# Two-layer graph attention: layer 1's exponentials made in layer 0 and read back from DRAM, and list work reordered

## The chip, the cores and the metric

The kernel runs on one core of a Trainium2 chip. The metric is the device time of one launch in microseconds; before the change the median of 3 runs is 1829.27 us (1828.33 to 1834.35). The engines are named as in the profile: PE (TensorE, matrix products; PEld its weight loads), DVE (VectorE), ACT (ScalarE), POOL (GpSimd) and SP (SyncE, which here only issues DMAs).

## What is computed

The input is a feature matrix `x` of 3327 x 1024 and a sparse symmetric adjacency matrix `adj` of 3327 x 3327 with its diagonal set. Two layers of graph attention follow one another, each with a residual and a layer norm:

```python
# layer 0: 8 heads of 128 columns
h = (x @ W0).reshape(C, 8, 128)
e = alpha_src[:, :, None] + alpha_dst[:, None, :]      # per head, from h . a_src and h . a_dst
e = where(e >= 0, e, 0.2 * e);  e = where(adj == 0, -inf, e)
x = layernorm(x + softmax(e) @ h)
# layer 1: one head of 1024 columns
h = x @ W1;  f1 = h @ a1;  f2 = h @ a2
e = leaky_relu(f1 + f2.T, 0.2);  scores = where(adj > 0, e, -9e15)
x = layernorm(x + relu(softmax(scores, axis=1) @ h))
```

The exponential of a leaky sum is split: up to a factor that cancels in the softmax, the weight of source j for target i is max(r_i * a_j, b_j), with r_i = exp(0.8 s_i), a_j = exp(d_j) and b_j = exp(0.2 d_j). So each layer needs one r for each target (and head), and two numbers for each source.

## The kernel before, in words

The 3327 rows are padded to 26 tiles of 128 (`NT`, `P`). There are three stages.

**Projections and lists** (the first block under `manual_schedule`). For each tile, `flip` transposes x on PE, `project` multiplies it by W0 in three column chunks (`CUTS0`), `keep` evicts the chunks on ACT and stores the tile's rows, with their source factors appended, to `h0_d` in DRAM. Beside it the generator `listing` turns each tile's adjacency rows into lists of neighbours: for each tile 17 columns of 128 source indices and target numbers (`idx`, `tgt`), four blocks of four groups and an end block. One round of `listing` works on several tiles at once: `keys` and `columns` (DVE) for tile t+1, `give`, `take` and `sources` (PE, ACT, DVE) for tile t, `ends` and `ends2` for tile t+3, and `count(t + 4)`, which clears the diagonal of a tile's mask on POOL (L342), sums the mask on ACT (L346), packs it on DVE (L353), and requests a later mask from POOL's queue (L531). `pace`, called after every second step of a projection, advances `listing` by a fixed quota (`slots`), and from tile 13 on also `sums_so_far`, which makes part of layer 0's sums for the first 13 tiles. Since the program is written in a fixed order, every engine takes its instructions in the order in which these generators emit them.

**Layer 0** (`pipeline` with `Layer0` items; tiles 13 to 25 alternate with tiles 0 to 12). A late item has blocks 0 to 4, an early one blocks 2 to 4. For each block POOL issues four indirect DMAs (one for the end block) that gather 128 rows each from `h0_d` into a ring of five buffers; `weights` makes the block's weights on DVE (L1093, L1094, L1098) and a copy on ACT (L1096); `sums` multiplies on PE (L1129; L1118 for the end block). `own` adds the target's own row: an Exp on ACT (L1065), three DVE operations (L1066 to L1068), then eight operations on ACT for late items (L1076) or on DVE for early ones (L1072). `finish` is a generator of five steps: the denominators (DVE L1151, PE L1152), the division and residual (L1155 to L1161), the layer norm (`norm_steps`: bn_stats L217, the square root on ACT L220, L224), and two dot products (L1168) that give layer 1's scores, whose exponentials (ACT L1173, L1174) are appended to the row before it goes to `y_d` in DRAM (SP, L1175).

**Layer 1** (`Target` items, in order of tiles). A block is again four gathers, now from `y_d`, the weights on DVE (L1223, L1224, L1226) and products on PE in three column chunks (L1235). `prepare` is called for the next item in the middle of the current one: it transposes the target scores on PE (L1191), takes their Exp on ACT (L1193), makes the marks on DVE (L1033, L1037) and requests the residual rows (SP, L1198). The transposed scores, their exponentials and the products of DVE all lie in one PSUM tile, `way`. `own` takes a second Exp of the same scores by column (L1204). `close` divides (L1249, L1252); `finish` transposes the result on PE with a copy on ACT (`turned`, L199), multiplies by W1 (L1267) and adds the residual (L1270), and `settle` is the layer norm with the store.

The table `plans` says which unfinished items advance after each block. A pair such as (2, 1) means: one step of the item two back, then one step of the item one back; the entry in front is for the start of an item, before its own work is emitted.

Of the kernel before, what the change touches and what calls it, by code (L numbers as in the profile page):

```python
# [14 lines left out]
OP = mybir.AluOpType  # L15
# [11 lines left out]
def kernel(  # L27
# [97 lines left out]
    idx = const.tile([P, NT, NB], I32, name="idx")  # L125
    tgt = const.tile([P, NT, NB], F32, name="tgt")
    wt1 = const.tile([P, KT, D], F32, name="wt1")
    half_d = [scratch.tile([P, D], F32, name=f"half_d{t}") for t in range(EARLY)]
    dens = const.tile([P, EARLY, H], F32, name="dens")
    io_t = const.tile([P, P], F32, name="io_t")  # L130
# [183 lines left out]
    class Edges:  # L314
# [10 lines left out]
        def factors(self):  # L325
# [6 lines left out]
            nc.gpsimd.tensor_copy(mv[:, 1, :], r[:, 1, :])  # L332
            nc.gpsimd.tensor_tensor(mv[:, 2, :], r[:, 1, :], mv[:, 1, :], OP.subtract)

        def words(self, ad, junk):

            sbuf, ph, t = self.ph.sbuf, self.ph, self.t  # L340
            own = ad[:, t * P : (t + 1) * P].bitcast(mybir.dt.int8)
            nc.gpsimd.affine_select(  # L342
                out=own, in_=own, pattern=[[1, P]], compare_op=OP.not_equal, fill=0.0, base=0, channel_multiplier=-1
            )
            for n in range(2):
                nc.scalar.activation(junk, ad[:, n * THR : (n + 1) * THR], AF.Copy, accum_out=self.d[:, n : n + 1])  # L346
            self.deg_b = sbuf("deg_b", [P, 2], 4, dt=BF16)
            nc.scalar.activation(self.deg_b, self.d, AF.Copy)
            w = ad.bitcast(I32)
            for n in range(3):  # L350
                m = WD >> n
                half = sbuf(f"wd{n}", [P, m], 4 if n == 2 else 1, dt=I32)
                nc.vector.scalar_tensor_tensor(  # L353
                    half, w[:, m:], 1 << n, w[:, :m], op0=OP.logical_shift_left, op1=OP.bitwise_or
                )
                w = half
            self.bytes = w.bitcast(U8)
# [152 lines left out]
    with ExitStack() as own, tc.manual_schedule():  # L510
# [39 lines left out]
        def keep(t, c):  # L550
# [12 lines left out]
            if kept[t] == 3:  # L563
                nc.sync.dma_start(h0_d[t * P : (t + 1) * P, :HW0], hts.pop(t))

        def count(t):
            if t < NT:
                lists[t].words(ads.pop(t), junk)
                if t:
                    load_mask(t + 2)  # L570

        def listing():

            for t in range(-1, NT):
                old, new = lists[t] if t >= 0 else None, lists[t + 1] if t + 1 < NT else None
                for s in range(4):
                    if old and s:
                        old.give(s - 1)
                    if new:
                        (new.keys, new.columns)[s // 2](s % 2)  # L580
                    if s == 1 and 2 < t + 3 < NT:
                        lists[t + 3].ends(tri_b)
                    if s == 3 and 2 < t + 3 < NT:
                        lists[t + 3].ends2(all_b)
                    yield
                if old:
                    old.give(EB - 1)
                    old.give(EB)
                    old.take()
                if new:  # L590
                    new.ways()
                count(t + 4)
                yield
                if old:
                    old.sources()
                    yield
                while new and t + 1 not in scored:
                    yield
                if new:
                    new.places()  # L600
                    yield
                    new.spread()
                    yield

        scored, kept, soon = set(), {}, []
        steps, slots, done = listing(), [0, 0], [0]

        def pace():
# [214 lines left out]
        )  # L823
        all_b = pool.tile([P, P], BF16, bufs=1, name="all_b")
        nc.vector.tensor_copy(all_b, tri)
        count(0)
        for _ in range(2):
            next(steps)
# [8 lines left out]
        project(1, 2, False)  # L837
        keep(1, 2)
        lists[0].ends2(all_b)
        lists[1].ends(tri_b)  # L840
        flip(3, 0)
        load_x(5)
        count(2)

        done[0], slots[:] = 4, [9, (NT - 3) * 12 + 13]
        project(2, 2, True, lambda: flip(3, 1))
        keep(2, 2)
        flip(4, 0)
        lists[1].ends2(all_b)
        lists[2].ends(tri_b)  # L850
        project(3, 2, True, lambda: flip(4, 1))
        keep(3, 2)
        lists[2].ends2(all_b)
        for t in range(3, NT):
            load_x(t + 3)
# [27 lines left out]
                )  # L883
            if t == NTH:
                soon.append(sums_so_far())
            for c in (0, 1):
                project(t, c)
                keep(t, c)
            if t + 2 < NT:
# [65 lines left out]
    def sparse(own):  # L955
# [3 lines left out]
        srcs = near + [pool.tile([P, NG, HG], F32, bufs=1, name=f"src{n}") for n in range(HB, NS)]  # L959
        ends = [pool.tile([P, 1, HG], F32, bufs=1, name=f"end{n}") for n in range(2)]  # L960
        r1 = Rows(pool, 1)

        ys = [pool.tile([P, HW], F32, bufs=1, name=f"y{n}") for n in range(3)]
        for y in ys:
# [75 lines left out]
        class Layer0:  # L1040
# [107 lines left out]
            def finish(self):  # L1148
# [23 lines left out]
                        yield  # L1172
                nc.scalar.activation(row[:, D + 1 : D + 2], r1.d[:, t, :], AF.Exp)  # L1173
                nc.scalar.activation(row[:, D + 2 : D + 3], r1.d[:, t, :], AF.Exp, scale=SLOPE)  # L1174
                nc.sync.dma_start(y_d[t * P : (t + 1) * P, :HW], row)  # L1175
                stored.add(t)

        class Target:

# [7 lines left out]

            def prepare(self):
                t = self.t
                tr = way[:, 3 * P :]  # L1190
                nc.tensor.transpose(tr, r1.s[:, t, :].to_broadcast([P, P]), ident)  # L1191
                self.r = way[:, ((t + 1) % 2) * P : ((t + 1) % 2 + 1) * P].rearrange("p (g t) -> p g t", g=NG)
                nc.scalar.activation(  # L1193
                    self.r.rearrange("p g t -> p (g t)"), tr, AF.Exp, scale=1 - SLOPE
                )
                self.oh, self.oh2 = marks(t)
                self.res = ys[self.n % 3]
                nc.sync.dma_start(self.res, y_d[t * P : (t + 1) * P, :HW])  # L1198

            def own(self):  # L1200

                t, res = self.t, self.res
                es = self.es = sbuf("es1", [P, 2], 2)
                nc.scalar.activation(es[:, 1:], r1.s[:, t, :], AF.Exp, scale=1 - SLOPE)  # L1204
                nc.vector.scalar_tensor_tensor(
                    es[:, 1:], res[:, D + 1 : D + 2], es[:, 1:], res[:, D + 2 : D + 3], op0=OP.mult, op1=OP.max
                )
                nc.vector.tensor_tensor(es[:, :1], es[:, 1:], loop[:, t : t + 1], OP.mult)

# [70 lines left out]
        def pipeline(items, fetches):  # L1280

            left, sums_of, sent = [], set(), [0]
            plans = {
                len(Target.blocks): ((), (1,), (1,), (1,), (1,), (1,)),
                len(Target.blocks) - HB: ((), (1, 1), (1, 1), (1,)),
                Target: ((2,), (2, 1), (2, 1), (1, 1), (1, 1), (1,)),
            }

# [32 lines left out]
            for i, it in enumerate(items):  # L1321
# [4 lines left out]
                for j, b in enumerate(it.blocks):  # L1326
                    if j == 0 and i:
                        items[i - 1].close()
                        if turn:
                            for _ in left[i - 1]:  # L1330
                                pass
                            send()
                            it.weights(b)
                        rest(i, 0)
# [185 lines left out]
```

## Time and profile before

| | us |
|---|---|
| median of 3 runs | 1829.27 |
| profiled execution, its own time | 1945.79 |
| span of its instructions | 1944.1 |
| PE busy | 1633.7 (84% of the span) |
| DVE busy | 1184.5 (61%) |
| POOL busy | 1092.2 (56%) |
| ACT busy | 573.4 (29%) |
| table loads on ACT: L220 / L1173 / L1193 | 50, 26 and 23 of 1.283 each |
| indirect DMAs (POOL) | 884, about 1 each |

The profile is of one execution, which took 1945.79 us, 6% more than the median of the timed runs. Its page gives the span in 40 equal slices (48.6 us each), each digit the busy share of an engine in tenths; `PEclk` is the share of full speed that PE's clock was granted, `DMA` the mean busy share of the core's 16 DMA engines. A row of a group has the line, the engine, the operation and its tiles, the count, busy time and mean duration, then the engine's idle time ahead of it and what ended it. In a timeline a row has its start in us, its duration in us, and in brackets how long the engine had been idle and what released it. Line numbers are those of the kernel before. Idle time of an engine that sets no end costs nothing.

### The profile page before, as it was taken

The page shows a single profiled execution, that of the slowest core. Times are in us where ns is not written, and L with a number is a line of the kernel's source. Part 1 is how long each engine was busy: PE and PEld are TensorE (multiplying, and loading weights), DVE is VectorE, ACT ScalarE, POOL GpSimd, SP SyncE. Part 2 cuts the span into 40 slices and gives each one's busy share as a digit, 9 for nine tenths or more (in the row PEclk, how much of TensorE's full clock was granted, in tenths as well). Part 3 has the DMA queues.
Part 4 walks back from the last instruction along what each step waited for, and adds up shares of the span by engine and source line. Part 5 has one row for each costly group of instructions (what it writes and reads, how often), then busy time and mean ns, then how long its engine had stood idle before and what let it go on. Part 6 is the DMA issues. An engine that isn't in the chain of part 4 may idle for free.

```text
span 1944.1 us, 35431 instructions
## 1 busy us (share of the span) xinstructions
PE 1633.7 (84%) x13168; PEld 919.9 (47%) x13168; DVE 1184.5 (61%) x3261; ACT 573.4 (29%) x1565; POOL 1092.2 (56%) x1580
## 2 busy tenths in 40 slices
PE   8699989989994777777777665798989999899988
PEld 5466556655563554554455442243434434333433
DVE  6699988777765776777777774243444344434342
ACT  5656554444321222222222121022122221222121
POOL 4433346656555666666666555565656666565640
PEclk9899999999996878888878877899999999999999
DMA  6555779887779999999999998899999999899980
GB/s 178 91 130 114 144 152 293 255 249 238 247 271 349 381 391 393 383 393 371 402 386 386 374 313 301 310 374 340 346 350 369 335 394 342 331 362 340 325 302 33
DMA packets 183364, 585.16 MB, mean 301 GB/s; under 512 B 36168, under 2 KB 42824, under 8 KB 183182
## 3 DMA queue, kind: packets, MB, share of 16 engines
q0 software_dynamic: 131056, 457.74, 68.4%
q1 hardware_dynamic: 52126, 125.06, 17.2%
q8 instruction: 107, 1.75, 0.4%
q14 instruction: 75, 0.61, 0.1%
HBM read 586.09 MB, written 51.22 MB: 328 GB/s over the span
## 4 chain that ended last, share of the span: by engine, by line
PE 43%; issue 10%; DVE 6%; ACT 4%; DMA 4%; POOL 1%; another core or an unknown queue 0%; DVEq 0%; ACTq 0%; POOLq 0%
PE mm L1267 17%; PE acc L1235 13%; PE acc L1129 8%; PE acc L1110 2%; DMA src<-h_d,idx 2%; PE tr L196 1%; ACT L1193 1%; PE acc L1118 1%; DVE e L1098 1%; ACT own L1076 1%; DMA near<-h_d,idx 1%; DVE pr L982 1%; DVE st L217 1%; ACT L220 1%; DMA src<-y_d,idx 1%
## 5 line engine op out<-in xcount | busy, mean ns | idle before, releaser
L542 PE MATMUL mm<-wt,xT 128*128 128x347 f32 (+1 forms) x1248 | 416.6, 475 | 6.8 <-ACT ht L561 3.3
L1267 PE MATMUL mm<-wt,xT 128*128 128x512 f32 x832 | 395.5, 613 | 2.6 <-issue 2.3
L1017 POOL DMA_INDIRECT src<-y_d,idx x248 | 249.1, 1005 | 166.8 <-PE acc L1235 71.0
L542 PEld LDWEIGHTS mm<-wt,xT 128*128 128x128 f32 x1248 | 228.5, 195 | 118.3 <-issue 19.7
L1017 POOL DMA_INDIRECT src<-h_d,idx x184 | 196.5, 1068 | 121.3 <-PE acc L1129 35.8
L1267 PEld LDWEIGHTS mm<-wt,xT 128*128 128x128 f32 x832 | 152.3, 193 | 211.5 <-issue 206.7
L1270 DVE SCALAR_TENSOR_TENSOR o<-mm,y 128x512 f32<-128x512 f32 x52 | 36.0, 692 | 322.2 <-PE acc L1235 126.4
L1017 POOL DMA_INDIRECT near<-y_d,idx x168 | 169.5, 1009 | 108.7 <-PE acc L1235 48.3
L1129 PE MATMUL acc<-src,e 128*32 128x128 f32 x2944 | 161.3, 324 | 52.1 <-issue 47.5
L1017 POOL DMA_INDIRECT near<-h_d,idx x120 | 130.6, 1088 | 82.4 <-PE acc L1129 31.0
L1235 PE MATMUL acc<-src,es 128*32 128x341 f32 x1488 | 130.6, 485 | 41.8 <-DVE es L1226 31.8
L1129 PEld LDWEIGHTS acc<-src,e 128*32 128x32 f32 x2944 | 111.5, 130 | 113.4 <-issue 93.8
L1098 DVE TENSOR_TENSOR e<-oh,way 128x1024 f32<-128x1024 f32 x104 | 127.1, 1222 | 59.3 <-ACT w L1096 43.1
L1129 PE MATMUL acc<-near,e 128*32 128x128 f32 x2048 | 116.0, 333 | 48.7 <-issue 34.8
L199 ACT ACTIVATE xT<-tr 128x512 f32<-128x512 f32 x104 | 62.1, 598 | 299.9 <-PE tr L196 151.6
L1129 PEld LDWEIGHTS acc<-near,e 128*32 128x32 f32 x2048 | 79.7, 133 | 93.7 <-issue 84.4
L1096 ACT ACTIVATE w<-way 128x32 f32<-128x32 f32 x104 | 20.3, 195 | 351.4 <-DVE way L1094 186.6
L1249 ACT ACTIVATE z<-y,ri 128x342 f32<-128x342 f32 (+1 forms) x78 | 39.5, 569 | 277.0 <-issue 121.6
L1235 PE MATMUL acc<-near,es 128*32 128x342 f32 (+1 forms) x1008 | 85.8, 469 | 21.3 <-DVE es L1226 14.0
L629 POOL DMA_INDIRECT near<-h_d,idx x76 | 82.1, 1080 | 31.5 <-issue 22.9
L1235 PEld LDWEIGHTS acc<-src,es 128*32 128x32 f32 x1488 | 44.4, 114 | 115.0 <-issue 61.1
L346 ACT ACTIVATE junk<-ad 128x1664 uint8<-128x1664 uint8 x52 | 83.8, 1611 | 16.2 <-POOL ad L342 14.8
(242 smaller groups left out, 2587.8 us busy)
## 6 DMA issues: line engine op xcount, KB each, us to landing
h_d<-ht SPq DMA_DIRECT2D x26, 520.0 KB
own<-h_d SPq DMA_DIRECT2D x26, 520.0 KB
y_d<-y SPq DMA_DIRECT2D x26, 514.0 KB
y<-y_d SPq DMA_DIRECT2D x26, 514.0 KB
x<-in_x_dram SPq DMA_DIRECT2D x25, 512.0 KB
y<-in_x_dram SPq DMA_DIRECT2D x25, 512.0 KB
out_dram<-o SPq DMA_DIRECT2D x25, 512.0 KB
ad<-in_adj_dram POOLq DMA_DIRECT2D x25, 415.9 KB
```

The source lines that it names most:

```text
L199: nc.scalar.activation(part, tr, AF.Copy)
L346: nc.scalar.activation(junk, ad[:, n * THR : (n + 1) * THR], AF.Copy, accum_out=self.d[:, n : n + 1])
L542: nc.tensor.matmul(acc, xT[t][:, k, :], wt[:, k, CUTS0[c] : CUTS0[c + 1]], start=k == 0, stop=k == KT - 1)
L629: nc.gpsimd.indirect_dma_start(out=src[n % 3][:, g, :], out_offset=None, in_=h0_d[:THR, :], in_offset=bass.IndirectOffsetOnAxis(ap=idx[:, ...
L1017: nc.gpsimd.indirect_dma_start(out=s[:, g, :w], out_offset=None, in_=table[:n, :], in_offset=bass.IndirectOffsetOnAxis(ap=idx[:, t, b * NG ...
L1098: nc.vector.tensor_tensor(e, oh.unsqueeze(2).to_broadcast([P, ng, H, wide]), wp.unsqueeze(3).to_broadcast([P, ng, H, wide]), OP.mult,)
L1110: nc.tensor.matmul(self.acc[j - 1].rearrange("p h d -> p (h d)"), ident, self.h[:, (j - 1) * HALF : j * HALF], start=False, stop=False,)
L1129: nc.tensor.matmul(self.acc[h // 4][g * GT : (g + 1) * GT, h % 4, :], e[:, g, h, :], rowsof[:, g, h, :], start=first and h % 4 == 0, stop= ...
L1235: nc.tensor.matmul(self.acc[c][to, :m], es[:, g, :], s[:, g, CUTS[c] : CUTS[c + 1]], start=b == 0, stop=b == EB,)
L1249: nc.scalar.activation(z[:, cut], self.res[:, cut], AF.Copy, scale=ri[:, 1:2])
L1267: nc.tensor.matmul(acc, xT[:, k, :], wt1[:, k, half], start=k == 0, stop=k == KT - 1)
L1270: nc.vector.scalar_tensor_tensor(o[:, half], acc, 0.0, res[:, half], op0=OP.max, op1=OP.add)
```

## The change

It has two halves. First, `r`, the exponential of the target scores of layer 1, is made in layer 0. `finish` of a `Layer0` item takes the Exp by column into a kept tile `grow`, and gains a sixth step: PE transposes that column (broadcast over 128 columns), ACT copies one row of the result to SBUF, and SP stores it as one line of 512 bytes, `row_d[t]`, in DRAM. In layer 1, `prepare` reads that line back into all 128 partitions with one DMA, in place of the transpose L1191 and the Exp L1193, and `own` reads `grow` in place of the Exp L1204. The tile `r` thereby moves from PSUM (`way`) to SBUF (`rr`). The plans call the sixth step at the start of an item, for the item two back.

Second, in the list work, the clearing of a mask's diagonal leaves `words` and becomes `clear`, emitted for tile t+4 with the third of a round's first four steps (and for tiles 0 to 2 at the start); `count(t + 4)` moves from the middle of a round to its end; `places` and `spread` share a step; the first projections of tile 3 and some `ends` are emitted in another order, with the pacing quota set to match.

```diff
--- before.py
+++ after.py
@@ -125,6 +125,7 @@
     idx = const.tile([P, NT, NB], I32, name="idx")
     tgt = const.tile([P, NT, NB], F32, name="tgt")
     wt1 = const.tile([P, KT, D], F32, name="wt1")
+    row_d = [scratch.tile([1, P], F32, name=f"row_d{t}") for t in range(NT)]
     half_d = [scratch.tile([P, D], F32, name=f"half_d{t}") for t in range(EARLY)]
     dens = const.tile([P, EARLY, H], F32, name="dens")
     io_t = const.tile([P, P], F32, name="io_t")
@@ -332,16 +333,19 @@
             nc.gpsimd.tensor_copy(mv[:, 1, :], r[:, 1, :])
             nc.gpsimd.tensor_tensor(mv[:, 2, :], r[:, 1, :], mv[:, 1, :], OP.subtract)
 
-        def words(self, ad, junk):
-
-
-
-
-            sbuf, ph, t = self.ph.sbuf, self.ph, self.t
-            own = ad[:, t * P : (t + 1) * P].bitcast(mybir.dt.int8)
+        def clear(self, ad):
+
+            own = ad[:, self.t * P : (self.t + 1) * P].bitcast(mybir.dt.int8)
             nc.gpsimd.affine_select(
                 out=own, in_=own, pattern=[[1, P]], compare_op=OP.not_equal, fill=0.0, base=0, channel_multiplier=-1
             )
+
+        def words(self, ad, junk):
+
+
+
+
+            sbuf = self.ph.sbuf
             for n in range(2):
                 nc.scalar.activation(junk, ad[:, n * THR : (n + 1) * THR], AF.Copy, accum_out=self.d[:, n : n + 1])
             self.deg_b = sbuf("deg_b", [P, 2], 4, dt=BF16)
@@ -563,8 +567,14 @@
             if kept[t] == 3:
                 nc.sync.dma_start(h0_d[t * P : (t + 1) * P, :HW0], hts.pop(t))
 
+        def clear(t):
+            if t < NT and t not in cleared:
+                cleared.add(t)
+                lists[t].clear(ads[t])
+
         def count(t):
             if t < NT:
+                clear(t)
                 lists[t].words(ads.pop(t), junk)
                 if t:
                     load_mask(t + 2)
@@ -580,6 +590,8 @@
                         (new.keys, new.columns)[s // 2](s % 2)
                     if s == 1 and 2 < t + 3 < NT:
                         lists[t + 3].ends(tri_b)
+                    if s == 2 and t >= 0:
+                        clear(t + 4)
                     if s == 3 and 2 < t + 3 < NT:
                         lists[t + 3].ends2(all_b)
                     yield
@@ -589,7 +601,6 @@
                     old.take()
                 if new:
                     new.ways()
-                count(t + 4)
                 yield
                 if old:
                     old.sources()
@@ -598,11 +609,12 @@
                     yield
                 if new:
                     new.places()
-                    yield
                     new.spread()
                     yield
-
-        scored, kept, soon = set(), {}, []
+                count(t + 4)
+                yield
+
+        scored, cleared, kept, soon = set(), set(), {}, []
         steps, slots, done = listing(), [0, 0], [0]
 
         def pace():
@@ -823,6 +835,8 @@
         )
         all_b = pool.tile([P, P], BF16, bufs=1, name="all_b")
         nc.vector.tensor_copy(all_b, tri)
+        for t in range(3):
+            clear(t)
         count(0)
         for _ in range(2):
             next(steps)
@@ -837,19 +851,21 @@
         project(1, 2, False)
         keep(1, 2)
         lists[0].ends2(all_b)
-        lists[1].ends(tri_b)
         flip(3, 0)
         load_x(5)
+        lists[1].ends(tri_b)
         count(2)
 
-        done[0], slots[:] = 4, [9, (NT - 3) * 12 + 13]
+        done[0], slots[:] = 4, [4, (NT - 3) * 12 + 8]
         project(2, 2, True, lambda: flip(3, 1))
         keep(2, 2)
+        lists[1].ends2(all_b)
         flip(4, 0)
-        lists[1].ends2(all_b)
-        lists[2].ends(tri_b)
         project(3, 2, True, lambda: flip(4, 1))
         keep(3, 2)
+        lists[2].ends(tri_b)
+        project(3, 0)
+        keep(3, 0)
         lists[2].ends2(all_b)
         for t in range(3, NT):
             load_x(t + 3)
@@ -883,7 +899,7 @@
                 )
             if t == NTH:
                 soon.append(sums_so_far())
-            for c in (0, 1):
+            for c in (0, 1)[t == 3 :]:
                 project(t, c)
                 keep(t, c)
             if t + 2 < NT:
@@ -959,6 +975,7 @@
         srcs = near + [pool.tile([P, NG, HG], F32, bufs=1, name=f"src{n}") for n in range(HB, NS)]
         ends = [pool.tile([P, 1, HG], F32, bufs=1, name=f"end{n}") for n in range(2)]
         r1 = Rows(pool, 1)
+        grow = pool.tile([P, NT], F32, bufs=1, name="grow")
 
         ys = [pool.tile([P, HW], F32, bufs=1, name=f"y{n}") for n in range(3)]
         for y in ys:
@@ -1172,8 +1189,15 @@
                         yield
                 nc.scalar.activation(row[:, D + 1 : D + 2], r1.d[:, t, :], AF.Exp)
                 nc.scalar.activation(row[:, D + 2 : D + 3], r1.d[:, t, :], AF.Exp, scale=SLOPE)
+                nc.scalar.activation(grow[:, t : t + 1], r1.s[:, t, :], AF.Exp, scale=1 - SLOPE)
                 nc.sync.dma_start(y_d[t * P : (t + 1) * P, :HW], row)
                 stored.add(t)
+                yield
+                tr = bank("T", [P, 4, P], "tr")
+                nc.tensor.transpose(tr[:, 0, :], grow[:, t : t + 1].to_broadcast([P, P]), ident)
+                line = sbuf("line", [1, P], 2)
+                nc.scalar.activation(line, tr[:1, 0, :], AF.Copy)
+                nc.sync.dma_start(row_d[t], line)
 
         class Target:
 
@@ -1187,11 +1211,11 @@
 
             def prepare(self):
                 t = self.t
-                tr = way[:, 3 * P :]
-                nc.tensor.transpose(tr, r1.s[:, t, :].to_broadcast([P, P]), ident)
-                self.r = way[:, ((t + 1) % 2) * P : ((t + 1) % 2 + 1) * P].rearrange("p (g t) -> p g t", g=NG)
-                nc.scalar.activation(
-                    self.r.rearrange("p g t -> p (g t)"), tr, AF.Exp, scale=1 - SLOPE
+                self.r = sbuf("rr", [P, P], 2).rearrange("p (g t) -> p g t", g=NG)
+                of = row_d[t][:, :]
+                nc.sync.dma_start(
+                    self.r.rearrange("p g t -> p (g t)"),
+                    bass.AP(tensor=of.tensor, offset=of.offset, ap=[[0, P], [1, P]]),
                 )
                 self.oh, self.oh2 = marks(t)
                 self.res = ys[self.n % 3]
@@ -1201,9 +1225,8 @@
 
                 t, res = self.t, self.res
                 es = self.es = sbuf("es1", [P, 2], 2)
-                nc.scalar.activation(es[:, 1:], r1.s[:, t, :], AF.Exp, scale=1 - SLOPE)
                 nc.vector.scalar_tensor_tensor(
-                    es[:, 1:], res[:, D + 1 : D + 2], es[:, 1:], res[:, D + 2 : D + 3], op0=OP.mult, op1=OP.max
+                    es[:, 1:], res[:, D + 1 : D + 2], grow[:, t : t + 1], res[:, D + 2 : D + 3], op0=OP.mult, op1=OP.max
                 )
                 nc.vector.tensor_tensor(es[:, :1], es[:, 1:], loop[:, t : t + 1], OP.mult)
 
@@ -1281,8 +1304,8 @@
 
             left, sums_of, sent = [], set(), [0]
             plans = {
-                len(Target.blocks): ((), (1,), (1,), (1,), (1,), (1,)),
-                len(Target.blocks) - HB: ((), (1, 1), (1, 1), (1,)),
+                len(Target.blocks): ((2,), (1,), (1,), (1,), (1,), (1,)),
+                len(Target.blocks) - HB: ((2,), (1, 1), (1, 1), (1,)),
                 Target: ((2,), (2, 1), (2, 1), (1, 1), (1, 1), (1,)),
             }
 
@@ -1327,8 +1350,8 @@
                     if j == 0 and i:
                         items[i - 1].close()
                         if turn:
-                            for _ in left[i - 1]:
-                                pass
+                            for _ in range(5):
+                                next(left[i - 1])
                             send()
                             it.weights(b)
                         rest(i, 0)
```

## The prediction, made before the result was known

> **What bounds the kernel now.** I read the page's forty slices first, then busy time by stretch, then who waited for whom on TensorE in each stage, then the timeline at the places those waits named.
>
> The slices show three stages: projections and edge lists to slice 11 (about 595 us), layer 0's sums to slice 23 (about 1190 us), layer 1 after that.
>
> ```profile
> PEclk9899999999996878888878877899999999999999
> DMA  6555779887779999999999998899999999899980
> ```
>
> TensorE's granted clock is low in the middle stage only, and there the DMA engines are full. By stretch (length, busy us of PE, PEld, DVE, ACT, POOL, then granted clock, DMA share, GB/s):
>
> ```profile
> 600.00:1100.00 500.00, 374.03 (x4973) 249.16 (x4965) 372.71 (x960) 111.71 (x307) 318.04 (x297) 0.84 1.00 387
> ...
> 1250.00:1850.00 600.00, 554.18 (x3114) 237.12 (x3113) 241.99 (x718) 127.41 (x219) 374.51 (x374) 0.98 0.94 350
> ```
>
> Layer 1 is TensorE's: 554 of 600 us, with DMA close behind at 0.94 (the fullest 50 us stretch of the run reads 1.02, which I take for saturation). Nearly all of TensorE's idle time there has one name (total us, times, longest):
>
> ```profile
> PE acc L1235 <- DVE es L1226: 44.6, 19, 2.8
> ```
>
> The timeline of one target shows where it is from. ScalarE's rows (start, duration):
>
> ```profile
> 1382.15 0.60 ACT L199 ACTIVATE xT<-tr 128x512 f32<-128x512 f32 x1 [7.18 <-PE mm L1267]
> 1382.76 1.28 ACT L220 ACT_TABLE_LOAD   x1
> 1384.06 0.20 ACT L220 ACTIVATE sg<-sg 128x1 f32<-128x1 f32 x1
> 1384.28 1.28 ACT L1193 ACT_TABLE_LOAD   x1
> 1385.57 0.26 ACT L1193 ACTIVATE way<-way 128x128 f32<-128x128 f32 x1
> ```
>
> and what they release on VectorE and then TensorE:
>
> ```profile
> 1385.86 0.30 DVE L1223 TENSOR_TENSOR way<-way,near 128x128 f32<-128x128 f32 x1 [3.44 <-ACT way L1193]
> ...
> 1386.88 1.93 PE L1235 MATMUL acc<-near,es 128*32 128x341 f32 x24 [2.73 <-DVE es L1226]
> ```
>
> The square root of the layer norm and the exponential for the next target each load a table. VectorE's weights for a block of the current target wait for that exponential, since both are in the tile `way`, and TensorE waits for the weights.
>
> **Layer 1, part by part.** Removed per target: the transpose L1191 (about 0.2 us of TensorE's time), the Exp L1193 (0.26), both table loads (1.28 each; with no Exp left in the layer the root's table stays), and the one-column Exp L1204. VectorE is free at 1382.42 (L1037 ends), so its three operations could end at 1383.5, before TensorE's own matmuls run out at 1384.14: the 2.73 us vanish whole. Summing TensorE's gaps between L1267 and L1235 from 1240 us on gives 24 gaps, 54.6 us; the transposes add 26 x 0.2 = 5. Ceiling: 60 us.
>
> Here a rule of the Trainium skill is weighed: ScalarE: Activation LUTs, section What ACT_TABLE_LOAD costs, gives 1283 ns and a drain of about 1380 more, 2.66 us a switch. The load agrees (1283 ns on all rows). The drain isn't there: from the end of the copy (1382.75) to the end of the Exp (1385.83) are 3.08 us, two loads and two activations. By the rule each target would carry 2.76 us more to remove, 66 us in 24 targets; I use the row.
>
> The cap is DMA. At 0.94 of 1.02, the 600 us from 1250 can't fall below 553: 47 us. The change adds a broadcast load per target (128 packets of 512 bytes). The nearest rows are the `re` loads, 128 packets of 544 bytes, 30 ns each in the packet records: 128 x 30 / 16 engines = 0.24 us, 26 times 6 us. Net cap 41 us, plus the two gaps (5.5 us) past 1850, where no gather runs. I take 44, with 30 and 60 as ends. The broadcast is issued on SP ahead of L1198 (1380.07) and is first needed when the next target's first weights are made, at 1393.27: 13 us. The `re` loads landed in a median of 6.9 us, 13.5 at worst, so that is hidden; behind it on SP is only L1198's load (landing 6.4), not used before the next target's start.
>
> **The turn to layer 1.** TensorE waited 9.0 us at 1212 for L1191, for VectorE's use of `way`. That goes, but the gathers of the first targets, which VectorE waited for (15.5 us), come next. I take 3 of 0 to 9.
>
> **Layer 0.** Added per item: an Exp of one column beside L1173 and L1174 (the same table, starts 0.1 us apart), and as a sixth step, put ahead of the next item's work, a transpose (0.14 + 0.27), ScalarE's copy of one line (L1096's 0.2), and a 512-byte store on SP. None of it is large; the order is what costs. The copy makes ScalarE wait for TensorE, and queued behind it are `own`'s Exp L1065, L1076 and the copy L1096, on which VectorE and then TensorE wait:
>
> ```profile
> 919.34 0.20 ACT L1173 ACTIVATE y<-sd 128x1 f32<-128x1 f32 x1 [1.13 <-DVE pr L1168]
> 919.45 0.18 ACT L1174 ACTIVATE y<-sd 128x1 f32<-128x1 f32 x1
> 919.55 0.19 ACT L1065 ACTIVATE es<-sd 128x8 f32<-128x8 f32 x1
> 920.44 2.45 ACT L1076 ACTIVATE own<-own,es 128x128 f32<-128x128 f32 x8 [0.70 <-DVE es L1066]
> ```
>
> ```profile
> 924.14 0.27 DVE L1151 TENSOR_TENSOR met<-den,meets 32x128 f32<-32x128 f32 x1
> ...
> 924.46 0.38 PE L1152 MATMUL den<-heads,met 32*128 32x8 f32 x2 [2.67 <-DVE met L1151]
> ```
>
> TensorE's largest idle group in this stage is this one: 45 us before L1152 in 14 waits. Between L1174 and L1065 now come Exp 0.1, transpose 0.41, copy 0.2 and two hand-offs of about 0.1: 0.9 us. Comparing L1174's end with the end of TensorE's last matmul of the item (L1122) at 25 boundaries, TensorE is 2.2 to 6.3 us behind at nine. There ScalarE would wait for it: at 902.09, say, L1065 would run near 902.8 in place of 896.77. L1151 then follows 5.1 us after (as at 940.5 to 945.6), not at 902.32, and TensorE, done with its block at 906.4, waits until about 908.2, some 2 us. Sum: 16 x 0.9 + 9 x 2 = 32 us if all of it is on the path. It need not be: the DMA at 1.00 sets nearly the same pace, and in an execution with a better clock it sets it alone. Nothing here can gain. Between 0 and 45 I take 18, the middle of the sum. SP waits for the line too, with the next `re` load behind it; that load has some 17 us until it is used.
>
> **The lists.** TensorE is busy 435 of 470 us from 100 to 570, so at most 35 can come back. VectorE's wait for the cleared mask,
>
> ```profile
> DVE wd L353 <- POOL ad L342: 57.0, 13, 6.9
> ```
>
> goes, since the clearing moves ahead of POOL's waits for ScalarE (L330 waited 101 us for L329). But TensorE's gaps that name VectorE are only 8.1 us (L659 <- L435) and 3.8. Against it, `places` and `spread` now stand in one step, so ScalarE's copies L447 (1.6 us for four) wait for VectorE's 1.3 us directly, with the evictions L561 behind them. The early clear passes no new wait: its mask was requested two rounds (over 40 us) before. The counts keep their work (2 x 1.6 us of ScalarE and the DMA of the next mask), later in the round. Bounds: 15 gained, 10 lost; I take 4 gained.
>
> **Sum.** 44 + 3 - 18 + 4 = 33 us of the profiled execution's 1945.8, or 1.7%. The median is 1829.3, 116 us below it; the trace cannot show where that execution lost those. I carry the share: 1829.3 x (1 - 33/1945.8) = 1798.
>
> **Rivals.**
> (1) The sum as above, 1783 to 1815. Chance 0.50.
> (2) The added chain in layer 0 is hidden and layer 1 isn't capped by DMA: 60 + 3 + 4 = 67, 1766 (1758 to 1783). For it: timed executions are shorter, so their clock or DMA was better. Against: DMA 0.94. Chance 0.22.
> (3) Layer 0 gives back all of it: 41 gained against 32 to 45 lost, 1822 to 1834. Chance 0.13.
> (4) Slower, by one mechanism: the granted clock in layer 0. TensorE: Matmul & The Clock Gate, section HAM oscillation, says that idle gaps over about 3.4 us halve the clock, which speaks against this change. The trace fits it: 0.84 where gaps reach 3.8 us, 0.98 in layer 1 where they end at 2.8. The waits at L1152 (3.3 us) would become 4.2. If that takes the clock from 0.84 to 0.77, TensorE's 374 us of 500 become 408: over 595 us 40 more, on top of the 32: 72 lost against 51 gained, 1849. It decides once layer 0 loses over 51 us (2 us an item). By the rows alone (no change of clock) that isn't reached. Chance 0.12.
> (5) It does not do what it says: the broadcast lands late or table loads stay, and layer 1 keeps its gaps. 1825 to 1845. Chance 0.03.
>
> **Numbers.** This measurement can tell about 0.3% (5.5 us) from no change. Faster by more: all of (1) and (2), a third of (3): 0.76. Within: most of the rest of (3): 0.10. Slower: (4), (5) and an edge of (3): 0.14. The range of 1766 to 1832 leaves out half of (2), (4) and (5), 0.2 or a little more.
>
> **What would show it.** Right: L1193 gone, one or two table loads after 1190 us, L1235's waits for `es` below 10 us, layer 1 some 45 us shorter at a DMA share near 1.0, and ScalarE waiting for the new transpose with L1152's waits longer. Wrong: a DMA share still at 0.94 with new TensorE gaps in layer 1, or layer 0 longer by over 40 us, or a list stage that moved by more than 15 us either way.

## The result, and the profile after

The changed kernel takes 1802.74 us (median of 4 runs, 1800.32 to 1803.67), where the kernel before takes 1830.01 in the same series (1828.33 to 1834.35): a ratio of 0.9849, 95% interval 0.9832 to 0.9865, 27 us less. Forecast were 1798 and a range of 1766 to 1832. The number is near, but the parts that it was added up from are not: layer 1 was to bring 44 us and the lists 4, and the stages show nearly the reverse.

The execution that was profiled before the prediction (1945.79 us) is of a slower kind than the timed ones, and so are E4 to E9, which ran on another chip than E0 to E3 and beside which the kernel before itself took 1968.37 (E4 to E7) and 1931.05 us (E8, E9): each ratio is to the kernel before beside that run. The kernel before was therefore profiled once more (E0): 1831.36 us, span 1829.7. "Before" means E0's profile from here on, if nothing else is said. E10 and E11 ran on a third chip, where the kernel before took 1830.37. In the lines below, line numbers are those of each run's own kernel; a wait's row has its total in us, how many times, and the longest; `issue` is time in which the engine waited for nothing that the profile shows.

The slices of the changed kernel (45.0 us each), then two stretches of it (length, busy us of PE, PEld, DVE, ACT and POOL, granted clock, DMA share, GB/s):

```profile
PEclk9999999999996777877787777799999999999999
DMA  7455859999879999999999999899999999999990
```

```profile
600.00:1100.00 500.00, 354.23 (x5239) 267.05 (x5238) 390.91 (x1020) 127.94 (x369) 325.79 (x306) 0.77 1.01 396
1250.00:1700.00 450.00, 450.00 (x2577) 194.47 (x2575) 202.21 (x608) 54.01 (x111) 319.84 (x314) 1.00 1.02 396
```

The same two stretches of the kernel before, in E0:

```profile
600.00:1100.00 500.00, 342.76 (x5131) 257.28 (x5123) 396.69 (x1023) 114.90 (x312) 324.25 (x306) 0.78 1.01 399
1250.00:1700.00 450.00, 450.00 (x2608) 195.33 (x2603) 201.42 (x599) 105.07 (x180) 316.84 (x316) 1.00 1.01 395
```

Both kernels show one picture: in layer 0 DMA is full (1.01), in layer 1 PE is busy for all of 450 us and DMA is full as well. Only ACT changes, 105 to 54 us. PE's waits of 44.6 us for `es` (a block's weights), on which the prediction rests, are not in E0 at all: from 1250 to 1850 us its list of PE's waits is empty.

I cut both traces at the end of the last projection, at layer 0's first and last product with gathered rows (the end block's included), and at layer 1's first:

| us | before (E0) | after | difference | forecast |
|---|---|---|---|---|
| lists and projections, to the last projection | 564.4 | 536.2 | -28.2 | -4 |
| from there to layer 0's first product | 26.3 | 27.9 | +1.6 | |
| layer 0's products | 557.8 | 560.5 | +2.7 | +18 |
| turn to layer 1 | 11.1 | 10.2 | -0.9 | -3 |
| layer 1 to the end | 670.0 | 665.7 | -4.3 | -44 |

### The profile page after: what moved, and what is told of

The parts are those of the page before. It is cut to its first block, busy times and chain, and to the rows that moved or that the text cites. A ratio compares the mean times of both kernels' runs of the same rounds, so it can differ in the third digit from the quotient of the medians.

```text
span 1800.4 us, 35590 instructions
## 1 busy us (share of the span) xinstructions
PE 1549.4 (86%) x13168; PEld 913.4 (51%) x13168; DVE 1185.0 (66%) x3261; ACT 515.0 (29%) x1519; POOL 1110.4 (62%) x1580
## 4 chain that ended last, share of the span: by engine, by line
PE 57%; DVE 19%; DMA 12%; issue 6%; ACT 4%; POOL 2%; DVEq 0%; SPq 0%; ACTq 0%; POOLq 0%
PE mm L1290 21%; PE acc L1258 13%; PE mm L546 11%; DMA src<-h_d,idx 6%; PE acc L1146 3%; PE part L671 2%; DVE e L1115 2%; PE tr L197 2%; DMA near<-h_d,idx 2%; ACT junk L350 1%; DMA end<-h_d,idx 1%; DVE pr L1185 1%; DVE top L309 1%; DVE y L1178 1%; DMA wt<-in_L_gnn_W_dram 1%
## 5 line engine op out<-in xcount | busy, mean ns | idle before, releaser
L546 PE MATMUL mm<-wt,xT 128*128 128x347 f32 (+1 forms) x1248 | 410.6, 470 | 4.2 <-DMA wt<-in_L_gnn_W_dram 4.2
L1290 PE MATMUL mm<-wt,xT 128*128 128x512 f32 x832 | 387.6, 604 | 0.0
L1034 POOL DMA_INDIRECT src<-y_d,idx x248 | 253.0, 1020 | 120.8 <-PE acc L1258 35.5
L546 PEld LDWEIGHTS mm<-wt,xT 128*128 128x128 f32 x1248 | 226.1, 192 | 121.9 <-issue 23.6
L1290 PEld LDWEIGHTS mm<-wt,xT 128*128 128x128 f32 x832 | 149.7, 189 | 198.6 <-issue 193.6
L1115 DVE TENSOR_TENSOR e<-oh,way 128x1024 f32<-128x1024 f32 x104 | 126.9, 1221 | 59.4 <-ACT w L1113 51.2
L1258 PE MATMUL acc<-src,es 128*32 128x341 f32 x1488 | 122.8, 464 | 21.2 <-DVE es L1249 21.2
L1146 PE MATMUL acc<-src,e 128*32 128x128 f32 x2944 | 132.3, 354 | 0.2
L1146 PE MATMUL acc<-near,e 128*32 128x128 f32 x2048 | 94.7, 362 | 16.2 <-DVE e L1115 16.2
L1197 PE MATMUL tr<-ident,grow 128*128 128x128 f32 x26 | 11.4, 437 | 91.5 <-ACT grow L1192 91.5
```

Of the source, the lines that this page charges most:

```text
L546: nc.tensor.matmul(acc, xT[t][:, k, :], wt[:, k, CUTS0[c] : CUTS0[c + 1]], start=k == 0, stop=k == KT - 1)
L1034: nc.gpsimd.indirect_dma_start(out=s[:, g, :w], out_offset=None, in_=table[:n, :], in_offset=bass.IndirectOffsetOnAxis(ap=idx[:, t, b * NG ...
L1115: nc.vector.tensor_tensor(e, oh.unsqueeze(2).to_broadcast([P, ng, H, wide]), wp.unsqueeze(3).to_broadcast([P, ng, H, wide]), OP.mult,)
L1146: nc.tensor.matmul(self.acc[h // 4][g * GT : (g + 1) * GT, h % 4, :], e[:, g, h, :], rowsof[:, g, h, :], start=first and h % 4 == 0, stop= ...
L1258: nc.tensor.matmul(self.acc[c][to, :m], es[:, g, :], s[:, g, CUTS[c] : CUTS[c + 1]], start=b == 0, stop=b == EB,)
L1290: nc.tensor.matmul(acc, xT[:, k, :], wt1[:, k, half], start=k == 0, stop=k == KT - 1)
```

## The experiments

**E0 and E1: the kernel before once more, and the layer half alone.** E1 puts only the parts of the diff from `row_d` and `grow` to the plans into the kernel before; the lists stay as they were.

> The kernel before, profiled once more, for its stages in an execution near the timed median. My theory: the list stage ends near 570 us as in the first profile, layer 0's sums last some 550 us, and layer 1 from its first product to the end some 45 us longer than the 666 us after the change, so about 710. Rival (layer 1 was not where the time came from): layer 1 within 15 us of 666, and the lists or layer 0 longer than after by 20 us or more.

> Only the first half of the change: layer 1's exponentials made in layer 0, the list work as before. My theory (44 + 3 gained in layer 1 and the turn, 18 lost in layer 0): about 29 us of 1830 gained, so 1801, ratio 0.984. Rival (the gain is the list work's, layer 0 eats what layer 1 gains): 1825 or more, ratio 0.997 or above.

E0: 1831.36 us. E1: 1831.02 (14 runs) against 1831.38 (19 runs), ratio 1.0003 [0.9991, 1.0015]. The half from which I took 29 of 33 us brings nothing, and costs nothing. In E0 layer 1 takes 670.0 us, where my theory had 710. Layer 0's products take 559.3 us in E1 (557.8 in E0), layer 1 668.6: about 1.5 us lost and 1.4 gained.

Why there is nothing to gain shows in ACT's timeline of one target in E0, at the place that the prediction showed for the other execution:

```profile
1417.13 0.60 ACT L199 ACTIVATE xT<-tr 128x512 f32<-128x512 f32 x1 [3.62 <-PE tr L196]
1417.74 1.28 ACT L220 ACT_TABLE_LOAD   x1
1419.04 0.20 ACT L220 ACTIVATE sg<-sg 128x1 f32<-128x1 f32 x1
1419.26 1.28 ACT L1193 ACT_TABLE_LOAD   x1
1420.56 0.26 ACT L1193 ACTIVATE way<-way 128x128 f32<-128x128 f32 x1
```

and in PE's and VectorE's at the same place. PE's rows have none of the brackets that a wait would leave:

```profile
1416.49 0.60 PE L196 MATMUL tr<-ident,z 128*128 128x128 f32 x4
...
1418.99 3.70 PE L1267 MATMUL mm<-wt,xT 128*128 128x512 f32 x8
1422.62 1.65 PE L1235 MATMUL acc<-near,es 128*32 128x341 f32 x20
```

```profile
1421.52 0.29 DVE L1226 TENSOR_TENSOR es<-way,oh 128x128 f32<-128x128 f32 x1
```

The chain is the one that I described, with both table loads and the same durations, but the copy L199 starts when PE's transposes end (1417.09). VectorE's last operation (L1226) ends at 1421.81, and PE comes to it at 1422.62: 0.8 us to spare. In the execution of 1945.79 us L199 began at 1382.15, 3.6 us after its transposes had ended (1378.54):

```profile
1377.94 0.60 PE L196 MATMUL tr<-ident,z 128*128 128x128 f32 x4
```

Take 0.8 us of spare time from those 3.6, and 2.8 are left; PE's wait there was 2.73.

**E2: the list half alone.** All of the diff except what E1 has.

> Only the second half: masks cleared ahead, counts last in a round, the rest as before. My theory: 4 us gained, 1826, ratio 0.998. Rival: the lists carry the gain, 1803 to 1810, ratio 0.985 to 0.989.

Measured: 1801.8 us (5 runs), ratio 0.9848 [0.9829, 0.9867], the same as the whole change. Its last projection ends at 533.9 us (E0: 564.4), and layers 0 and 1 are unchanged (557.5 and 670.6). So the list half is the whole gain. PE's waits in the first 100 us of E0:

```profile
PE xp L466 <- ACT mvg L447: 8.0, 1, 8.0
PE dd L362 <- ACT cnt L388: 5.3, 2, 4.5
PE avs L749 <- DMA near<-in_L_gnn_a_src_dram: 4.2, 1, 4.2
PE mm L542 <- DMA wt<-in_L_gnn_W_dram: 3.8, 1, 3.8
```

and in E2:

```profile
PE tr L196 <- ACT xT L199: 5.4, 1, 5.4
PE avs L760 <- DMA near<-in_L_gnn_a_src_dram: 4.3, 1, 4.3
PE mm L545 <- DMA wt<-in_L_gnn_W_dram: 2.1, 1, 2.1
PE dd L365 <- ACT cnt L391: 0.5, 1, 0.5
```

Of 21.3 us, 12.3 are left. The other place is from 300 to 530 us, where E0 has

```profile
PE part L659 <- DVE mvs L435: 12.6, 4, 4.9
PE part L659 <- DVE e L650: 2.6, 2, 1.9
PE xp L466 <- ACT mvg L447: 2.3, 1, 2.3
```

and E2 none of the three. In busy time by stretch, first E0, then E2 (0 to 100, 100 to 300, 300 to 530 us; together PE has 473.1 us in E0, 498.2 in E2):

```profile
0.00:100.00 100.00, 78.69 (x267) 49.68 (x268) 62.64 (x168) 56.25 (x190) 44.61 (x154) 0.90 0.58 131
100.00:300.00 200.00, 184.44 (x902) 120.89 (x902) 183.95 (x529) 118.82 (x377) 81.76 (x324) 1.00 0.68 150
300.00:530.00 230.00, 209.97 (x1965) 138.35 (x1964) 176.83 (x482) 103.76 (x325) 138.26 (x299) 0.97 0.82 255
```

```profile
0.00:100.00 100.00, 87.76 (x328) 55.62 (x329) 71.65 (x197) 60.46 (x211) 51.80 (x168) 0.98 0.67 149
100.00:300.00 200.00, 185.26 (x962) 122.73 (x964) 183.85 (x522) 120.98 (x375) 83.00 (x316) 0.98 0.70 156
300.00:530.00 230.00, 225.14 (x2141) 149.90 (x2134) 190.66 (x524) 107.68 (x342) 157.11 (x313) 0.99 0.87 273
```

PE has done 9.1, 0.8 and 15.2 us more work in these stretches, 25 of the 30.5 us. The granted clock over the 530 us is 0.97 in E0 and 0.98 in E2; by an estimate from these two, 1% of 473 us, it could account for 5 us of the gain. VectorE's wait for the cleared mask, E0's row first, then E2's, nearly goes:

```profile
DVE wd L353 <- POOL ad L342: 55.2, 12, 7.1
DVE wd L356 <- POOL ad L338: 2.6, 1, 2.6
```

By the order of the program, the operations that PE's early sums of layer 0 (L659) wait for stand behind it on VectorE. E4 to E9 look at how far the two belong together.

**E3: no wait of ScalarE for PE in layer 0.** In the changed kernel the transpose, the copy and the store of a line are replaced by one store of the column straight from `grow`, 128 pieces of 4 bytes:

```diff
+                of = row_d[t][:, :]
+                nc.sync.dma_start(
+                    bass.AP(tensor=of.tensor, offset=of.offset, ap=[[1, P], [1, 1]]), grow[:, t : t + 1]
+                )
                 yield
-                tr = bank("T", [P, 4, P], "tr")
-                nc.tensor.transpose(tr[:, 0, :], grow[:, t : t + 1].to_broadcast([P, P]), ident)
-                line = sbuf("line", [1, P], 2)
-                nc.scalar.activation(line, tr[:1, 0, :], AF.Copy)
-                nc.sync.dma_start(row_d[t], line)
```

> The changed kernel without the sixth step's work: SP stores the column of exponentials to DRAM as 128 packets of 4 bytes, with no transpose and no copy, so ScalarE never waits for TensorE there. The output is the same. My theory (the wait costs layer 0 about 18 us): 1785, ratio to before 0.975, with layer 0's sums some 18 us shorter than the 560.5 after. Rival (DMA sets layer 0's pace and hides the wait): 1800 to 1805, as after the change.

Measured: 1964.84 us, ratio 1.0735 [1.0708, 1.0762]. The wait is gone and the kernel is far slower: layer 0's products take 709.6 us in place of 560.5. From 600 to 1100 us:

```profile
600.00:1100.00 500.00, 284.59 (x4151) 213.84 (x4143) 303.25 (x790) 95.53 (x273) 250.53 (x237) 0.75 1.01 305
```

DMA is as full as before (1.01) but moves 305 GB/s, not 396. So E3 doesn't say what the wait was worth: it brought in a larger cost. It does show that layer 0 gets longer when the DMA engines move less in the same time.

What the wait is worth is read from PE's waits between 600 and 1100 us, in the kernel before (E0)

```profile
PE den L1152 <- DVE met L1151: 85.4, 23, 5.2
PE acc L1129 <- issue: 30.6, 12, 3.3
PE acc L1129 <- DVE e L1098: 29.0, 10, 4.2
```

and in the changed one:

```profile
PE tr L1197 <- ACT grow L1192: 88.3, 23, 5.8
PE den L1169 <- DVE met L1168: 51.1, 24, 3.9
PE acc L1135 <- DVE e L1115: 3.3, 3, 1.3
```

The added transpose has become PE's largest wait, 88 us, yet the sum of the three is 142.7 us where it was 145.0, and PE is idle for 146 of the 500 us where it was 157. With DMA at 1.01 in both, the new wait has taken up idle time that lay elsewhere.

**E4 to E9: the list half in parts**, each put into the kernel before. E4 and E8 only move the clearing:

```diff
+                    if s == 2 and t >= 0:
+                        clear(t + 4)
...
+        for t in range(3):
+            clear(t)
```

E5 only puts the counts last, and E6 does both:

```diff
-                count(t + 4)
                 yield
...
                     new.places()
-                    yield
                     new.spread()
                     yield
+                count(t + 4)
+                yield
```

E7 and E9 have the other order of the opening alone, with its quota:

```diff
-        done[0], slots[:] = 4, [9, (NT - 3) * 12 + 13]
+        done[0], slots[:] = 4, [4, (NT - 3) * 12 + 8]
...
+        project(3, 0)
+        keep(3, 0)
...
-            for c in (0, 1):
+            for c in (0, 1)[t == 3 :]:
```

> The kernel before with one edit of the list work: masks cleared ahead (for tile t+4 with the third step of a round, for tiles 0 to 2 at the start); the counts stay in the middle of a round. Theory A (the clearing is the cause: VectorE, then TensorE wait for POOL's clear, 57 us in the list stage before): most of the 29 us, 1805 to 1812. Theory B (the place of the counts is the cause: ScalarE's 3.7 us of counting stand ahead of the four copies of spread and of evictions, for which TensorE waits): 1826 to 1831. Theory C (the opening's order is the cause): 1826 to 1831.

> The kernel before with one edit: the counts last in a round, places and spread in one step; the clearing still at the head of the counts. Theory A: 1826 to 1831. Theory B: 1805 to 1815. Theory C: 1826 to 1831.

> Both edits of the two kernels before this one together, the opening as before. If the opening's order is worth what its gaps in TensorE say (21 us of gaps ahead of 100 us before, 12 in the list half: 9 us), 1811. Theory C: 1828. If the opening is worth nothing: 1802.

> The kernel before with the new order of the opening only (the first projection of tile 3 brought forward, two of the ends later, the pacing quota to match). By TensorE's gaps 9 us: 1822. Theory C (the opening is the cause): 1803. Theories A and B: 1822 to 1831.

> The kernel with only the masks cleared ahead once more, since the last four were measured where the kernel before itself took 1968 us and scattered by 1%. There the clear alone gave 0.986, the opening alone 0.987, the counts last 0.996: more than the whole list half (0.985) if added up. Where the kernel before takes 1830: theory A 1805 to 1812 (ratio 0.986 to 0.990), with the last projection at about 545 us in place of 564. If TensorE's gaps that name VectorE (15 us) are all it removes: 1815.

> The kernel with only the new order of the opening once more, for the same reason. By TensorE's gaps ahead of 100 us (21 us against 12): 1821, ratio 0.995, with the last projection some 9 us earlier. Theory C: 1803. If VectorE, not TensorE, limits the first 300 us (it is busy 184 of 200 us from 100 on), the time won at the opening is lost again behind it: 1828 to 1831.

| part | us | ratio, 95% interval | last projection ends | PE busy to 530 us |
|---|---|---|---|---|
| E4 clearing ahead | 1944.96 | 0.9859 [0.9806, 0.9911] | 546.6 | 487.3 |
| E8 the same again | 1911.46 | 0.9900 [0.9864, 0.9935] | 550.0 | 486.6 |
| E5 counts last | 1958.41 | 0.9958 [0.9938, 0.9977] | 579.8 | 466.2 |
| E6 both | 1947.60 | 0.9887 [0.9846, 0.9928] | 567.6 | 475.1 |
| E7 opening | 1942.95 | 0.9869 [0.9827, 0.9911] | 574.8 | 475.5 |
| E9 the same again | 1914.88 | 0.9976 [0.9952, 0.9999] | 570.6 | 473.5 |

The last two columns for the kernel before in its execution of 1945.79 us are 571.0 and 473.6. The times of these runs are a poor guide to the list stage: in the six traces layer 1, which none of the edits touches, takes from 708.6 to 766.6 us. So the last two columns count for more, though each is of one execution.

Only the clearing shortens the list stage alone, by 24 and 21 us in two traces, and its time is lower both times (1.4% and 1.0%), as theory A had it. PE's wait for `mvs` from 300 to 530 us, 8.1 us in the execution of 1945.79 us and 12.6 in E0, is 0 in E4 and 3.3 in E8, while the wait in the first 100 us stays (10.2 us for `mvg` in E4). In E4 VectorE's wait for the mask falls to

```profile
DVE wd L356 <- POOL ad L338: 15.7, 6, 6.7
```

in place of 55.2 us. But the mask's wait isn't tied to the one for `mvs` for certain: E5 has 38.6 us of the first and none of the second, and E7 and E9, where the mask's wait is whole (59.4 and 60.6 us), have 4.6 and 5.2 of the second. That the clearing shortens the stage is shown; by which wait is argued.

For the other two parts times and traces don't agree: E7's gain of 1.3% shrank to 0.2% in E9, and neither the opening (theory C) nor the counts (theory B) shortened the stage in their traces. Counts last makes it longer in its own trace, and in that of E6 most of the clearing's gain is gone, though E6's time is 1.1% lower; PE waits for the counts (`deg_b`) there, 28.4 us in E5 and 16.3 in E6 (but 14.4 in E2 too). E6's stage is 3 us shorter than the 571.0, E2's 30 us shorter than E0's; whether the opening and its quota make this difference is not settled. Clearing and opening without the counts was not tried.

**E10 and E11: a late ScalarE, with and without the Exp.** In both kernels four copies, used by nothing, stand in `prepare`, straight ahead of the Exp L1193 in the kernel before (E10) and of the request for the line in the changed one (E11):

```diff
+                slow = sbuf("slow", [P, HALF], 1, dt=BF16)
+                for _ in range(4):
+                    nc.scalar.activation(slow, wa[0][:, :HALF], AF.Copy)
```

> The kernel before, with four copies added on ScalarE straight ahead of the Exp L1193 of each target in layer 1 (their result is used by nothing; some 2 us together). Theory: in an execution near the median that Exp arrives about 0.8 us before TensorE needs the weights made from it, so 2.1 us of delay cost about 1.3 us a target, 26 x 1.3 = 34 us, about 1864 us where the kernel before takes 1830, and TensorE's gaps ahead of L1235 that name es come back. Rival: ScalarE's lateness costs nothing in layer 1, since TensorE or the DMA hides it whatever the state (within 5 us of before).

> The changed kernel with the same four copies on ScalarE at the same place in each target (ahead of the request for the line, with no Exp behind them). Theory: nothing that TensorE waits for stands behind them, so it stays within 5 us of the changed kernel, about 1803 us, 0.985 of before; the difference to the run with the copies in the kernel before is then what removing the Exp is worth when ScalarE is late. Rival: the copies cost through ScalarE's other work (the copy of the transposed result, the roots), and then this run is longer by as much as the other, some 34 us, about 1837.

E10: 1870.92 us against 1830.37, ratio 1.0215 [1.0198, 1.0232], 40.55 us more. E11: 1803.46, ratio 0.9852 [0.9835, 0.9868], the changed kernel's own time. In E10 the copies take 2.60 us, and the stall of the prediction is back (PE's waits from 1250 to 1850 us, then the rows around one of them):

```profile
PE acc L1238 <- DVE es L1229: 36.8, 22, 1.7
```

```profile
1406.76 0.60 ACT L199 ACTIVATE xT<-tr 128x512 f32<-128x512 f32 x1 [3.62 <-PE tr L196]
...
1408.78 2.60 ACT L1192 ACTIVATE slow<-wa 128x512 bf16<-128x512 f32 x4
...
1412.69 0.26 ACT L1196 ACTIVATE way<-way 128x128 f32<-128x128 f32 x1
```

```profile
1408.63 3.70 PE L1270 MATMUL mm<-wt,xT 128*128 128x512 f32 x8
1414.00 1.93 PE L1238 MATMUL acc<-src,es 128*32 128x341 f32 x24 [1.67 <-DVE es L1229]
```

The copies put the Exp off by 2.50 us (it begins 5.93 us after the copy L199 in place of 3.43), and that gives 1.67 us of wait: the spare time of this target is 0.8 us, as E0's rows had it. Layer 1 takes 710.5 us in place of 670.0, which is the difference in time. So the layer half does what it says. It removes a dependence that has 0.8 us to spare: in an execution like E0 that is worth nothing, and in the one lateness that was put in, 2.50 us, about 40 us.

## Why the number was near and the reasons were wrong

**Layer 1: 44 us forecast, 1 to 5 measured.** The mechanism was described rightly (E10 brings it out), but the stall is not in the executions whose time was to be forecast. The step that failed is "I carry the share". I had noted that the profiled execution was 116 us over the median and that the trace could not show where it lost them, and still took a stall of 54.6 us from it as a property of the kernel. Layer 1 alone is 76 us longer there than in E0 (746.1 against 670.0). The gain that is left is the transposes: 26 x 0.2 = 5 us of a PE that is never idle (1.4 us between E1 and E0, 4.9 between the whole change and E2). The sign of it was in the stretch that I showed: a DMA share of 0.94 and a clock of 0.98 in a stage that E0 runs at 1.01 and 1.00 (1250 to 1700 us). I read the first as room. The mean clock of the run gave no hint (0.918, and 0.912 in E0).

Nor was that execution a single oddity. The stall is in all six traces of E4 to E9 as well (18.9 to 33.0 us of PE's waits for `es` from 1250 to 1850 us; 39.1 in the first profile), and L199 begins over 1 us after its transposes end 20 to 23 times in layer 1 in each of these seven traces, but only once, near the start of layer 1, in each of E0, E1, E2 and the changed kernel. VectorE is late there too. Its L1270 follows products of PE that end at 1378.10 in the first profile and at 1416.65 in E0:

```profile
1379.31 0.69 DVE L1270 SCALAR_TENSOR_TENSOR o<-mm,y 128x512 f32<-128x512 f32 x1 [6.21 <-PE way L1191]
```

```profile
1416.69 0.69 DVE L1270 SCALAR_TENSOR_TENSOR o<-mm,y 128x512 f32<-128x512 f32 x1 [6.66 <-PE mm L1267]
```

That is 1.2 us later in the first profile, and 0.04 in E0. Two engines late behind PE would fit a cause on PE's side rather than ScalarE's, and the ends of PE's products are modelled in the profile; no run settles it, and the cause stays open. Whether the layer half gains on such a chip was not run.

**The cap by DMA.** "Net cap 41 us" used 0.94 of 1.02 as room. In E0 there is no room: 1.01. From 1200 to 1790 us VectorE's weights wait 23 times for the Exp (23.8 us) and 7 times for gathers (15.9 us) in E0. In the changed kernel they wait 31 times for gathers (77.3 us). After the turn PE waits for neither.

**The rule on table loads.** The row was the better guide: two loads and two activations take 3.08 us in the first execution and 3.09 in E0 (1417.73 to 1420.82), so the drain of about 1380 ns of the Trainium skill (ScalarE: Activation LUTs, section What ACT_TABLE_LOAD costs) shows in neither. With both loads in it, 2.57 us a target, the chain still ends 0.8 us before PE comes to it in E0, so removing them was worth nothing.

**Layer 0: 18 us lost forecast, 1 to 3 measured** (E1 1.5 over E0, the whole change 2.7 over E0 and 3.0 over E2). The waits came, in another place than I had put them: PE waits for ScalarE's `grow` at the transpose, and L1152's waits grew shorter, not longer. The sum of 16 x 0.9 and 9 x 2 us priced waits of PE in a stage in which the DMA engines set the pace. I had named that ("in an execution with a better clock it sets it alone") and then took 18, roughly the middle (it would be 16). A reading was wrong too: L1152 was not PE's largest idle group there, since the same list has 82.3 us in 176 short gaps before L1129 that name `issue`.

**The clock (rival 4)** did not decide anything: the granted clock from 600 to 1100 us is 0.78 before, with waits of PE up to 5.2 us, and 0.77 after, with waits up to 5.8, and layer 0 takes 3 us more.

**The lists: 4 us gained forecast (10 lost to 15 gained), 28 to 30 measured.** Two steps failed. I counted only PE's gaps "that name VectorE" as what the cleared mask could give back, 8.1 and 3.8 us, where the clearing alone shortened the stage by 21 and 24. And PE was idle 21.3 us in the first 100 us of E0 (the first profile has 77.9 busy of 100), a stretch that I left out altogether, starting at 100 us; the edits of the opening were given no price at all, and in E2 PE does 9 us more work there.

**The sum.** 33 us of the first execution were forecast, carried over as 31 of the median; 27 were measured. Layer 1 was too large by about 40, the lists too small by about 24, layer 0 too dear by 15: the errors cancel, so the right total was luck and has shown nothing about the steps.

## What to carry to other kernels

Before counting a stall, compare the profiled execution with the median; where it is some per cent longer, take the stage's DMA share and clock as a warning, and price a gain in the cases with and without the stall rather than carrying its share. Waits of an engine that doesn't bound a stage are neither a price nor a gain by themselves: layer 0 took 88 us of new waits of PE without getting longer by more than 3. In a stage whose order is written out by hand, count all idle time of the bounding engine, from the first microsecond on, and not only the gaps that name the edited operation.

## What was not expected of the hardware

The 128 pieces of 4 bytes of E3 cost 149 us in 26 items, 5.7 us each, for 512 bytes. Packets of 4 bytes are short in the records (9 ns in the median of 9445 in E3 between 600 and 1100 us, the store's among them; the changed kernel has 8880 others); the long ones are those of other traffic. In that stretch 821 of 30683 packets of gathered rows (4160 bytes) take over 1 us, where it is 26 of 39650 in the changed kernel; the median is 161 ns in both. The changed kernel's line of 512 bytes, written in one piece, brings no such tail.
